# A recurrent layer and a gated attention on one core: the value products move to the head of a step, ScalarE's transfers to 3 + 3 + 2

## The chip, the core and the metric

The kernel runs on one core of a Trainium2 chip. The core has five engines that run side by side and meet through semaphores: TensorE (PE; its weight loads are listed apart as PEld), VectorE (DVE), ScalarE (ACT), GpSimd (POOL) and SyncE (SP, which only issues transfers). Each engine works through its own list of instructions in order: an instruction that waits holds up all that stand behind it on that engine. SP and ACT both issue DMA transfers here.

The metric is the time of one execution in microseconds (us) on the device: the median of the runs. Beside it stands the profile of one execution, in which every instruction has a start and a duration.

## The reference

The input is x (2, 2048, 256) in float32. Two layers follow each other, each behind a layer norm and with its input added back.

```
x = x + rnn(layernorm(x))            # h = tanh(x Wi' + bi + h Wh' + bh), 128 steps and 64 sequences by name;
                                     # here 2 sequences of 2048 steps
q, k = (x @ Wq), (x @ Wk)            # 8 heads of 64
wv   = top2mask(x @ Ws) * sigmoid(x @ Ws)        # per head, 5 experts
v    = sum over e of wv[e] * (x @ Wv[e])
attn = softmax(q k' / 8) v                       # 2048 x 2048 scores per head
out  = sum over e of top2mask(x @ Wd)[e] * (attn @ Wo[e])
x = x + out
```

The second layer has 2 batches x 8 heads, each with 2048 queries against 2048 keys. It fills the span from about 400 us on and is what the change touches.

## The kernel before, in words

The first layer, the gates and the turned inputs are made in the first 400 us. From there one hand-written schedule runs: the block under `tc.manual_schedule()` at the end of the function fixes each engine's order of instructions.

**Units and steps.** A head's queries are cut in four blocks of 512 (`QB`); a head and a block are a unit u, 64 in all. A unit has four steps (`U_T = 4`), each for 128 queries of each of the block's tiles; a step is called W (or t), 256 of them and some more to drain. `T0` is the first step of a head (16 steps a head). In a step the scores come in two parts of 1024 columns. For each part: `scores` (PE, L486) into one of three PSUM buffers, `lowest` (DVE, L500; the scores are negated, so the minimum is what the exponential subtracts), `exponential` (ACT, L510), `turn` (DVE, L522: a transposition within 32 x 32 blocks into a tile `st` that holds two steps; there are two such tiles).

**Deals.** The transposed blocks must also change partitions. `deal` (L537) does that with DMA: sixteen transfers of 128 KB for each pair of steps, from `st` into `pt`, which holds a unit. Eight of them, `LOWER`, go out on SP at an even step right behind `turn(t - 1, 1)`. Eight, `UPPER`, go out on ACT between its exponentials: 3 behind the first exponential of the even step, 2 behind the second, 2 behind the first of the odd step, 1 behind the second. The sixteen are called a wave here, ACT's eight A1 to A8 and SP's S1 to S8. The wave that starts at a step W with W mod 4 = 0 completes a unit; that with W mod 4 = 2 holds its first half.

In the program that is built, the transfers of SP and ACT share eight completion semaphores, given out in turn. A transfer is issued only when the one before it on its semaphore, eight transfers earlier, has landed.

**Products.** `products(u, c)` (L547) multiplies `pt` of a unit with the values `v`, four matrix products a step over four steps (16 in all, each two records in the profile). Every one reads all four steps of the unit, so the first cannot start before the unit's last deal has landed. `LAG = 6` puts the first of unit u at the end of step 4u + 6, behind that step's scores. Then `take` (ACT, L557, at the head of step 4u + 10) brings the result to SBUF, `turn_back` (PE transposes, L597, and an ACT copy `at`, L601, at 4u + 10) turns it, and `close` (POOL, L608 to L624) scales it, applies the output gates and adds it to `y`.

**The lists START, MID and LATE.** Everything else is put with `at(W, place, f, ...)` into a list that the step runs at its head, its middle or its end: `keys` and `queries` of the next head (L398, L414 on PE, copies on ACT; START), `fetch` of stored expert values (SP, L459), `mix` and `mix_sum` (POOL, L469 to L478) that make `v` from them, `weigh` (five small stages on DVE, POOL, ACT that turn minima and sums into weights; `least` is stage 0, `rec` stage 3), and for the last head of a batch `turn_out`, `project_out` and `store` (PE L641, L654, ACT L644 and L647, DVE L661). During heads 2 to 5 of the first batch `experts` (PE L445 on `xs`, which `turned_in` loads with SP; ACT copy L452) makes the expert values of the second batch, two chunks every eight steps, and `keep_experts` stores them.

**One PSUM bank for the small things.** `misc` gives `pk`, `pq`, `pv`, `po`, `py` and `pz` one and the same bank (`bufs=1`). A PE instruction that writes one of them waits until the one before has been read by ACT or DVE. PE's list is in order, so whatever stands behind waits too.

**PE's order at a unit's border** is, by the code before: scores of step 4u + 10 (part 0, part 1), `turn_back(u)`, products of the next unit, START of step 4u + 11 (every fourth unit: `keys`), scores of step 4u + 11.

Of the kernel before, what the change touches and what calls it, by code (L numbers as in the profile page):

```python
# [20 lines left out]
def rnn_then_switchhead_kernel(  # L21
# [336 lines left out]


    U_T = 4  # L360
    LAG = 6
    H_T = NQ * U_T
    G = P // 32
    big = ctx.enter_context(tc.tile_pool(name="big", bufs=2))
# [9 lines left out]
    units = [(i, n) for i in range(len(heads)) for n in range(NQ)]  # L374
# [3 lines left out]
    HC = NCH // 2  # L378

    def weights(i):  # L380
        h = heads[i][1]
        w = ap.tile([P, 2, KC, DH], F32, tag="wqk", name=f"wqk{i}")
        for j, W in enumerate((Wq, Wk)):
            nc.sync.dma_start(
                out=w[:, j], in_=W[:, h * DH : (h + 1) * DH].rearrange("(c p) h -> p c h", p=P)
            )
        w_of[i] = w

    def keys(i, part):

        b, h = heads[i]
        if part == 0:
            k_of[i] = ap.tile([P, 2, QB], F32, tag="k", name=f"k{i}")
        pk = misc([P, 2, HC, 32], f"pk{i}_{part}")
        xc = xT_of[b].rearrange("p k (f c g n) -> p k f g c n", f=2, g=G, n=32)
        for kc in range(KC):
            for o in range(2):
                nc.tensor.matmul(  # L398
                    pk[o * DH : (o + 1) * DH],
                    lhsT=w_of[i][:, 1, kc, :],  # L400
                    rhs=xc[:, kc, part, 2 * o : 2 * o + 2],
                    start=kc == 0,
                    stop=kc == KC - 1,
                )
        nc.scalar.copy(k_of[i][:, part, :], pk.rearrange("p g c n -> p (g c n)"))

    def queries(i, part):

        b, h = heads[i]
        pq = misc([P, QB], f"pq{i}_{part}")  # L410
        for kc in range(KC):
            for o in range(2):
                n = 2 * part + o
                nc.tensor.matmul(  # L414
                    pq[o * DH : (o + 1) * DH, :],
                    lhsT=w_of[i][:, 0, kc, :],
                    rhs=xT_of[b][:, kc, n * QB : (n + 1) * QB],
                    start=kc == 0,
                    stop=kc == KC - 1,
                )  # L420
        q = ap.tile([P, QB], F32, tag="q", name=f"q{i}_{part}")
        qs = ap.tile([P, QB], F32, tag="qs", name=f"qs{i}_{part}")
        nc.scalar.mul(q, pq, -SCALE)
        nc.sync.dma_start(out=qs[0:DH, :], in_=q[DH:P, :])
        nc.sync.dma_start(out=qs[DH:P, :], in_=q[0:DH, :])
        q_of[i, 2 * part] = (q, qs)
        q_of[i, 2 * part + 1] = (qs, q)
# [11 lines left out]
    def experts(b, c):  # L439

        if c % 2 == 0:
            xq_of["x", b, c // 2] = ap.tile([P, 2, DH, E], F32, tag="xq", bufs=3, name=f"xw{b}_{c}")
        pv = misc([P, E, DH], f"pv{b}_{c}")
        for kc in range(KC):
            nc.tensor.matmul(  # L445
                pv.rearrange("p e k -> p (e k)"),
                lhsT=(xT_of[b][:, kc, c * P : (c + 1) * P] if b == 0 else xq_of["s", b, c][:, kc, :]),
                rhs=wv[:, kc].rearrange("p e k -> p (e k)"),
                start=kc == 0,
                stop=kc == KC - 1,  # L450
            )
        nc.scalar.copy(xq_of["x", b, c // 2][:, c % 2], pv.rearrange("p e k -> p k e"))  # L452

    def keep_experts(b, k):
        nc.sync.dma_start(out=xvd[b, k], in_=xq_of.pop(("x", b, k)))
# [86 lines left out]
    def products(u, c):  # L542
        i, _ = units[u]
        if c == 0:
            o_of[u] = ps_o.tile([P, QB], F32, tag="o", name=f"o{u}")
        o = c // HC
        nc.tensor.matmul(  # L547
            o_of[u][o * DH : (o + 1) * DH, :].rearrange("p (g r) -> p g r", r=32),
            lhsT=v_of[i][:, c, :],
            rhs=pt_of[u].rearrange("p g s c r -> p (g s) c r")[:, :, c, :],  # L550
            start=c % HC == 0,
            stop=c % HC == HC - 1,
        )

    def take(u):
        os = ap.tile([P, QB], F32, tag="os", bufs=1, name=f"os{u}")
        nc.scalar.copy(  # L557
            os.rearrange("p (s g r) -> p g s r", g=G, s=U_T),
            o_of.pop(u).rearrange("p (g s r) -> p g s r", g=G, s=U_T),
        )  # L560
        o_of["s", u] = os
        pt_of.pop(u)
# [101 lines left out]
    START, MID, LATE = 0, 1, 2  # L664
    todo = {}

    def at(W, place, f, *a):
        todo.setdefault((W, place), []).append(lambda: f(*a))

    for i, (b, h) in enumerate(heads):  # L670
        T0 = i * H_T
        fresh = h == 0
        if i > 0:
            at(T0 - 13, START, weights, i)
            at(T0 - 5 if fresh else T0 - 9, START, keys, i, 0)
            at(T0 - 4 if fresh else T0 - 7, START, keys, i, 1)
            at(T0 - 3, START, queries, i, 0)
        at(T0 + 4, START, queries, i, 1)
        for n, part in enumerate((0, 4, 1, 5, 2, 6, 3, 7)):
            W = T0 - 3 + n if i == 0 else T0 - 11 + 2 * n  # L680
            at(max(W, 0), LATE, fetch, i, part)
            at(max(W + 2, n), LATE, mix, i, part)
            at(max(W + 2, n), LATE, mix_sum, i, part)
        if h == H - 1 and b + 1 < B:
            at(T0 + 5, LATE, load_turned)
        if h == H - 6 and b + 1 < B:
            for c in range(NCH):
                W = T0 + 8 * (c // 2) + c % 2
                at(W, LATE, turned_in, b + 1, c)
                at(W + 2, START, experts, b + 1, c)  # L690
            for k in range(NCH // 2):
                at(T0 + 8 * k + 4, LATE, keep_experts, b + 1, k)
    for u, (i, n) in enumerate(units):
        b, h = heads[i]
        T1 = u * U_T + LAG + U_T
        for k in range(5):
            at(T1 - 6 + k, LATE, weigh, u, k)
        at(T1, MID, turn_back, u)
        at(T1, LATE, close, u)
        if h == H - 1:  # L700
            for s in range(U_T):
                c = n * U_T + s
                at(T1 + s, LATE, residual_in, b, c)
                at(T1 + 2 + s, START, turn_out, b, c)
                at(T1 + 2 + s, MID, project_out, b, c)
                at(T1 + 3 + s, LATE, store, b, c)

    with tc.manual_schedule():
        weights(0)
        keys(0, 0)  # L710
        queries(0, 0)
        keys(0, 1)
        for c in range(NCH):
            experts(0, c)
            if c % 2 == 1:
                keep_experts(0, c // 2)
        for W in range(NT + LAG + U_T + 8):
            t, u, j = W, (W - LAG) // U_T, (W - LAG) % U_T

            def extra(place):  # L720
                for f in todo.pop((W, place), []):
                    f()

            def upper(a, b, c, d):
                if t % 2 == 0 and 0 < t <= NT:
                    deal(t - 1, nc.scalar, UPPER[a:b])
                if t % 2 == 1 and 1 < t <= NT + 1:
                    deal(t - 2, nc.scalar, UPPER[c:d])

            if j == 0 and 0 < u <= len(units):  # L730
                take(u - 1)
            extra(START)
            if t < NT:
                scores(t, 0)
                lowest(t, 0)
            if 0 < t <= NT:
                turn(t - 1, 1)
                if t % 2 == 0:
                    deal(t - 1, nc.sync, LOWER)
            if t < NT:  # L740
                exponential(t, 0)
                scores(t, 1)
                lowest(t, 1)
            upper(0, 3, 5, 7)
            extra(MID)
            if t < NT:
                turn(t, 0)
                exponential(t, 1)
            upper(3, 5, 7, 8)
            if 0 <= u < len(units):  # L750
                for c in range(2):
                    for o in range(2):
                        products(u, o * HC + 2 * j + c)
            extra(LATE)
        assert not todo, todo.keys()

# [47 lines left out]
```

## Time and profile before

| | us |
|---|---|
| median of 3 runs | 2102.23 |
| runs | 2097.94 to 2102.54 |
| the profiled execution | 2105.63 |
| its span, first to last instruction | 2103.7 |
| PE busy | 1553.8 (74%) |
| DVE busy | 1462.6 (70%) |
| POOL busy | 917.5 (44%) |
| ACT busy | 814.2 (39%) |
| mean granted TensorE clock | 0.844 |

Busy time does not count the issuing of transfers, which holds ACT's list as well. A line of the profile names the source line, the engine, the operation and `out<-in` by the program's names. In an answer on waits, `PE o L547 <- DMA pt<-st: 97.8, 44, 6.9` reads: PE stood idle ahead of line 547 until a deal landed, 97.8 us in total, in 44 places, 6.9 us the longest. In a timeline a line starts with start and duration, and ends in brackets with the idle time ahead of it and what ended it. `xN` merges N neighbours of one kind; `ACTq` and `SPq` are the issuing of transfers.

### The profile page before, as it was taken

What the parts mean: (1) busy time and instruction counts of PE and PEld (TensorE: products, weight loads), DVE (VectorE), ACT (ScalarE), POOL (GpSimd) and SP (SyncE); (2) the same over time, 40 slices, a digit from 0 to 9 for tenths busy, and PEclk for the clock granted to TensorE, in tenths of its full rate; (3) what the DMA queues carried; (4) which work ended last, traced back from release to release, by engine and by line L of the source; (5) the groups of instructions that cost most, each with busy time, mean ns of one, the idle gap of its engine ahead of it and who ended that gap; (6) DMA issues with size and microseconds to landing.
All of it is one profiled execution on the core that took longest, in us unless ns stands there. A gap on an engine that the chain in (4) does not pass through costs nothing.

```text
span 2103.7 us, 21889 instructions
## 1 busy us (share of the span) xinstructions
PE 1553.8 (74%) x6226; PEld 608.0 (29%) x6226; DVE 1462.6 (70%) x2170; ACT 814.2 (39%) x1571; POOL 917.5 (44%) x1150
## 2 busy tenths in 40 slices
PE   5952223777878777777788799888878788878786
PEld 4852222222222222222222233222222222222233
DVE  8667775378766666666777676777778777777750
ACT  2530000345443444444444444444444444444441
POOL 0000000355555555544666544456556556565432
PEclk9975555989888888889899899888889888888897
DMA  3000000478776767776878877777777878777771
GB/s 104 1 14 30 30 30 25 135 203 232 206 194 175 202 182 203 194 189 186 215 202 206 224 206 198 218 207 203 192 205 213 208 205 217 198 193 206 200 202 41
DMA packets 161020, 352.04 MB, mean 167 GB/s; under 512 B 49344, under 2 KB 70656, under 8 KB 160768
## 3 DMA queue, kind: packets, MB, share of 16 engines
q1 hardware_dynamic: 110112, 215.70, 38.1%
q10 hardware_dynamic: 50784, 134.89, 24.1%
q8 instruction: 52, 0.85, 0.2%
q14 instruction: 72, 0.59, 0.1%
HBM read 57.89 MB, written 15.73 MB: 35 GB/s over the span
## 4 chain that ended last, share of the span: by engine, by line
PE 28%; DMA 26%; DVE 23%; SPq 5%; issue 5%; POOL 3%; ACT 3%; ACTq 2%; DVEq 0%; POOLq 0%
DMA pt<-st 23%; PE o L547 10%; DVE low L500 8%; DVE st L522 7%; PE s L486 7%; SPq L537 4%; PE pv L445 2%; ACTq L537 2%; PE pz L654 2%; PE pk L398 2%; DMA xs<-x2d 2%; PE pg L304 1%; ACT e L510 1%; DMA xq<-xvd 1%; PE pq L414 1%
## 5 line engine op out<-in xcount | busy, mean ns | idle before, releaser
L500 DVE TENSOR_REDUCE low<-s 128x1 f32<-128x1024 f32 x512 | 612.6, 1197 | 396.1 <-PE s L486 395.3
L510 ACT ACTIVATE e<-s,low 128x1024 f32<-128x1024 f32 x512 | 571.0, 1115 | 652.0 <-DVE low L500 385.3
L522 DVE STREAM_TRANSPOSE st<-e 128x1024 f32<-128x1024 f32 x512 | 631.3, 1233 | 82.2 <-DMA pt<-st 44.8
L547 PE MATMUL o<-pt,v 128*64 128x512 f32 x2048 | 580.3, 693 | 110.9 <-DMA pt<-st 97.8
L486 PE MATMUL s<-k,q 64*128 64x512 f32 x1024 | 547.7, 652 | 17.6 <-ACT e L510 17.6
L486 PE MATMUL s<-k,qs 64*128 64x512 f32 x1024 | 547.7, 652 | 13.3 <-ACT e L510 13.1
L469 POOL TENSOR_TENSOR xq<-xq,gates_all 128x640 f32<-128x640 f32 x128 | 190.7, 1489 | 399.2 <-DMA xq<-xvd 399.2
L608 POOL TENSOR_TENSOR at<-at,f 128x512 f32<-128x512 f32 x64 | 66.7, 1042 | 496.5 <-ACT at L601 496.5
L547 PEld LDWEIGHTS o<-pt,v 128*64 128x64 f32 x2048 | 142.6, 151 | 441.1 <-issue 405.5
L486 PEld LDWEIGHTS s<-k,q 64*128 64x128 f32 x1024 | 180.0, 200 | 207.1 <-issue 115.2
L486 PEld LDWEIGHTS s<-k,qs 64*128 64x128 f32 x1024 | 180.1, 200 | 194.4 <-issue 101.7
L478 POOL TENSOR_TENSOR v<-v,xq 128x128 f32<-128x128 f32 x384 | 199.8, 520 | 30.1
L624 POOL TENSOR_TENSOR y<-y,pro 128x1280 f32<-128x1280 f32 x56 | 162.4, 2900 | 4.4
L597 PE MATMUL po<-ident,os 128*128 128x128 f32 x256 | 49.3, 323 | 116.1 <-ACT os L557 109.0
L617 POOL TENSOR_TENSOR pro<-at,gates_all 128x1280 f32<-128x1280 f32 x56 | 130.9, 2338 | 4.4
L293 PE MATMUL tpc<-ident,xn 128*128 128x128 f32 x64 | 17.4, 427 | 151.3 <-DVE xn L141 146.0
L510 ACT ACTIVATION_READ_ACCUMULATOR e<-s,low 128x1 f32 x512 | 100.2, 196 | 0.0
L569 POOL TENSOR_TENSOR f<-least,low 128x8 f32<-128x8 f32 x64 | 12.8, 200 | 185.1 <-DVE least L567 185.1
L601 ACT COPY at<-po 128x512 f32<-128x512 f32 x64 | 37.5, 585 | 133.4 <-DMA xq<-xvd 54.1
L597 PEld LDWEIGHTS po<-ident,os 128*128 128x128 f32 x256 | 31.0, 157 | 167.0 <-ACT os L557 149.5
L297 ACT COPY xs<-tpc 128x256 f32<-128x256 f32 x16 | 6.0, 372 | 178.7 <-DVE xT L296 178.7
L398 PE MATMUL pk<-xT,wqk 128*64 128x512 f32 x256 | 66.9, 644 | 9.6 <-DMA wqk<-in_Wk 8.9
(107 smaller groups left out, 1278.1 us busy)
## 6 DMA issues: line engine op xcount, KB each, us to landing
pt<-st ACTq DMA_DIRECT2D x1024, 128.0 KB, 3.6
pt<-st SPq DMA_DIRECT2D x1024, 128.0 KB, 3.8
xq<-xvd SPq DMA_DIRECT2D x128, 320.0 KB, 4.3
qs<-q SPq DMA_DIRECT2D x64, 128.0 KB, 3.2
xvd<-xw SPq DMA_DIRECT2D x16, 320.0 KB, 3.1
x<-in_x SPq DMA_DIRECT2D x16, 256.0 KB, 5.7
x1d<-x SPq DMA_DIRECT2D x16, 256.0 KB, 2.0
z<-x1d SPq DMA_DIRECT2D x32, 128.0 KB, 2.9
```

The lines of the kernel that those rows point to most:

```text
L398: nc.tensor.matmul(pk[o * DH : (o + 1) * DH], lhsT=w_of[i][:, 1, kc, :], rhs=xc[:, kc, part, 2 * o : 2 * o + 2], start=kc == 0, stop=kc == ...
L469: nc.gpsimd.tensor_tensor(xq, xq, w.unsqueeze(2).to_broadcast([P, 2, DH, E]), ALU.mult)
L478: nc.gpsimd.tensor_tensor(v, v, xq[:, :, :, e], ALU.add)
L486: nc.tensor.matmul(ss[:, o, :], lhsT=q_of[i, n][o][half, s * P : (s + 1) * P], rhs=k_of[i][half, part, :], start=True, stop=True,)
L500: nc.vector.tensor_reduce(low_of[u][:, s, part : part + 1], s_of[t, part].rearrange("p o q -> p (o q)"), AX.X, ALU.min,)
L510: nc.scalar.activation(e_of[t, part], s_of.pop((t, part)), AF.Exp, bias=low_of[u][:, s, part : part + 1], scale=-1.0, accum_out=den_of[u][ ...
L522: nc.vector.transpose(st_of[t // 2][:, :, t % 2, part * HC : (part + 1) * HC, :].rearrange("p g c r -> p g (c r)"), e_of.pop((t, part)).re ...
L537: engine.dma_start(out=pt_of[u][32 * k : 32 * (k + 1), g, j : j + 2], in_=st_of[t // 2][32 * g : 32 * (g + 1), k],)
L547: nc.tensor.matmul(o_of[u][o * DH : (o + 1) * DH, :].rearrange("p (g r) -> p g r", r=32), lhsT=v_of[i][:, c, :], rhs=pt_of[u].rearrange("p ...
L597: nc.tensor.transpose(po[:, s].rearrange("p o k -> p (o k)"), os[:, s * P : (s + 1) * P], ident)
L617: nc.gpsimd.tensor_tensor(pr, at[:, :, 0, :].unsqueeze(2).to_broadcast([P, U_T, E, DH]), mask.unsqueeze(3).to_broadcast([P, U_T, E, DH]), ...
L624: nc.gpsimd.tensor_tensor(y, y, pr, ALU.add)
```

## The change

Five things change in the schedule; no instruction is added or taken away.

1. `LAG` is 7 and the products stand at the head of a step, behind START, ahead of the step's scores. On PE their place among the scores is the same as before. What is different: START's work of that step (`keys`, `queries`, `experts`, `turn_out`) now stands ahead of the products, not behind them.
2. `take(u)` stands behind the unit's last products in the same step, 4u + 10, and so behind START's copies on ACT, not ahead of them. The stages of `weigh` come one step later (`T1 - 5 + k`, with the same `T1`).
3. ACT's deals are split 3, 3, 2: A6 goes out ahead of the odd step's first exponential, A7 and A8 right behind it; none behind the second.
4. `fetch`, `mix` and `mix_sum` of the later heads come one step later; `weights` moves from START to LATE of the same step.
5. `experts` comes 5 steps behind `turned_in`, not 2; `keep_experts` 4 steps later than before.

```diff
-    LAG = 6
+    LAG = 7
...
-            at(T0 - 13, START, weights, i)
+            at(T0 - 13, LATE, weights, i)
...
-            W = T0 - 3 + n if i == 0 else T0 - 11 + 2 * n
+            W = T0 - 3 + n if i == 0 else T0 - 10 + 2 * n
...
                 at(W, LATE, turned_in, b + 1, c)
-                at(W + 2, START, experts, b + 1, c)
+                at(W + 5, START, experts, b + 1, c)
             for k in range(NCH // 2):
-                at(T0 + 8 * k + 4, LATE, keep_experts, b + 1, k)
+                at(T0 + 8 * k + 8, LATE, keep_experts, b + 1, k)
...
-        T1 = u * U_T + LAG + U_T
+        T1 = u * U_T + LAG + U_T - 1
         for k in range(5):
-            at(T1 - 6 + k, LATE, weigh, u, k)
+            at(T1 - 5 + k, LATE, weigh, u, k)
...
-            if j == 0 and 0 < u <= len(units):
-                take(u - 1)
             extra(START)
+            if 0 <= u < len(units):
+                for c in range(2):
+                    for o in range(2):
+                        products(u, o * HC + 2 * j + c)
+                if j == U_T - 1:
+                    take(u)
...
-            upper(0, 3, 5, 7)
+            upper(0, 3, 6, 8)
             extra(MID)
             if t < NT:
                 turn(t, 0)
                 exponential(t, 1)
-            upper(3, 5, 7, 8)
-            if 0 <= u < len(units):
-                for c in range(2):
-                    for o in range(2):
-                        products(u, o * HC + 2 * j + c)
+            upper(3, 6, 8, 8)
             extra(LATE)
```

## The prediction

> **What bounds the kernel now.** First the chain that ended last, by line, on the page.
>
> ```profile
> DMA pt<-st 23%; PE o L547 10%; DVE low L500 8%; DVE st L522 7%; PE s L486 7%; SPq L537 4%; PE pv L445 2%; ACTq L537 2%; PE pz L654 2%; PE pk L398 2%; DMA xs<-x2d 2%; PE pg L304 1%; ACT e L510 1%; DMA xq<-xvd 1%; PE pq L414 1%
> ```
>
> No engine is full; the chain alternates between deals in flight and the products behind them. The waits say who stands still meanwhile.
>
> ```profile
> DVE low L500 <- PE s L486: 395.3, 101, 43.1
> ...
> ACT e L510 <- DMA pt<-st: 107.2, 54, 5.6
> PE o L547 <- DMA pt<-st: 97.8, 44, 6.9
> ...
> PE pv L445 <- DMA xs<-x2d: 47.3, 8, 7.7
> ```
>
> The products wait 97.8 us for deals, and VectorE waits 395.3 us for scores, which stand behind those products on TensorE. ScalarE waits too: a deal whose semaphore is not free holds the exponential behind it. Next ScalarE's timeline over one completing wave (released at 1058.74, when VectorE's transposition 1057.51 + 1.23 ended).
>
> ```profile
> 1061.78 0.51 ACTq L537 DMA_DIRECT2D pt<-st  x1
> 1062.40 1.11 ACT L510 ACTIVATE e<-s,low 128x1024 f32<-128x1024 f32 x1 [0.51 <-DVE low L500]
> ...
> 1063.42 1.93 ACTq L537 DMA_DIRECT2D pt<-st  x2
> ...
> 1065.57 0.51 ACTq L537 DMA_DIRECT2D pt<-st  x1
> ...
> 1069.81 0.58 ACT L601 COPY at<-po 128x512 f32<-128x512 f32 x1 [1.47 <-issue]
> ```
>
> The lines are A5, the odd step's exponential, A6 and A7, A8, and the copy that frees the small PSUM bank. By the chain A7 went out at 1064.84, 0.02 us after an earlier deal had landed, and A8 landed at 1069.81. TensorE, the same moment:
>
> ```profile
> 1067.29 0.78 PE L597 MATMUL po<-ident,os 128*128 128x128 f32 x4 [2.50 <-ACT os L557]
> 1069.94 3.68 PE L547 MATMUL o<-pt,v 128*64 128x512 f32 x8 [1.88 <-DMA pt<-st]
> 1073.38 2.46 PE L398 MATMUL pk<-xT,wqk 128*64 128x512 f32 x8
> ```
>
> So a unit is a loop: scores, seven VectorE operations (7 us), a wave (11 us), products (3.7 us), sometimes a projection (2.2 us), scores. It takes 22.6 to 25 us in the plain stretches. VectorE's own work in it is 8 x (1.20 + 1.23) = 19.4 us; it has 3.4 to 5.8 us of slack, all at the unit's border.
>
> **The deals (change 3).** The hope in it is that the last deal lands earlier. A7 cannot leave before 1064.84, when its semaphore comes free. A8 then follows at the issue's 0.51 us, at 1065.37, not 1065.57: 0.2 us earlier. I read twenty more waves the same way: in nearly all A7 is held by S4, S5 or A4, landed 5.9 to 6.8 us into the wave. The price is ScalarE's: A6 left at 1063.42 and not at 1062.30 although ScalarE was free to issue, so it is held too, and now the exponential stands behind it and starts near 1064.0 instead of 1062.40, 1.6 us late. VectorE's slack at the border covers that; uncovered it would cost 1.6 us a unit. Which semaphores meet depends on the new order, which I can't see. Bounds for A8: 0.9 us earlier (if A7 and A8 go straight behind A6 and that exponential) to 0.8 us later (if A7 waits for S6, some 1 us behind S5). I take 0.15 us earlier, the row's nearest, over 30 plain units: **-5 us**, between -27 and +24.
>
> **Products and START (changes 1 and 2).** Ahead of scores nothing changes: products of a unit already stood between the scores of step 4u + 10 and those of 4u + 11. What changes is START.
>
> *Keys at the border.* At step T0 - 9 (mod 4: 3, the border) `keys` now stands ahead of the first products. It looks like free filling of the 1.88 us wait. But `pk` needs the one small bank, and the copy that frees it ran at 1069.81 to 1070.39, later than the products could start. So `pk` waits, and the products, whose deals have landed, wait behind it. The copy also comes later itself: it stands behind the next wave's first three deals, whose transposition is held by the late exponential (0.85 us). So `pk` starts at about 1071.2 where the products had started at 1069.94: 1.3 us. Would TensorE be quicker afterwards? The rows of a busy stretch (1.94 us for eight product records, 1.89 for eight of `pk`) give 3.83 us for both, a gain of 2 us against the 5.83 seen. The Trainium skill, TensorE: Matmul & The Clock Gate, section "What's actually happening", says that the gate opens after a stretch of busy time of about 3.4 us, not after a number of matmuls. Then whichever group comes first is slow and the sum stays 5.83; I take this, since the 3.68 us row above is such a first stretch. Ten heads outside the special stretches: **+13 us** (0 if the copy were early, 20 if it is 2 us late).
>
> *turn_out.* For the last head of the first batch each of 16 steps runs `py` (START), scores, `pz` (MID), products. Here the products filled the time in which VectorE emptied the bank:
>
> ```profile
> 1248.29 1.94 PE L547 MATMUL o<-pt,v 128*64 128x512 f32 x8
> 1250.16 0.55 PE L641 MATMUL py<-ident,y 128*128 128x128 f32 x3
> ```
> ```profile
> 1248.91 0.41 DVE L661 TENSOR_TENSOR z<-pz,z 128x256 f32<-128x256 f32 x1
> 1249.24 1.22 DVE L522 STREAM_TRANSPOSE st<-e 128x1024 f32<-128x1024 f32 x1
> 1251.82 1.22 DVE L500 TENSOR_REDUCE low<-s 128x1 f32<-128x1024 f32 x1 [1.35 <-PE s L486]
> ```
>
> `py` could start when z ends, 1249.32. Now: `py` 1249.35, products 1249.85 to 1251.7, scores 1.0 us later than before; and VectorE is already waiting for these scores (1.35 us). The other steps give 0.75 to 1.5 us. With four such steps in the second batch (the rest is drain, where no scores follow): 20 x 1.0 = **+20 us** (10 to 28).
>
> *take* behind START's copies: only `experts` has one there (0.42 us, eight times), covered by the deals' 2 us. Nothing, or 3 us.
>
> **Experts (change 5).** Before, `pv` comes two steps behind the load of `xs`, which SP issues behind eight deals:
>
> ```profile
> 766.58 2.47 PE L445 MATMUL pv<-wv,xs 128*128 128x320 f32 x4 [5.02 <-DMA xs<-x2d]
> ```
>
> VectorE stood 7.45 us there. The eight units with this take 29.1 to 31.0 us between transpositions that release their waves, against about 24.5 (plus 0.5 for the loads, which stay): 8 x 4.6 = **-37 us** (-30 to -42). With five steps the load is long there.
>
> The new places cost. Steps T0 + 8k + 5 meet `queries` of the next head (T0 - 3) four times: `pv`, then `pq`, one bank. `pq` waits for ScalarE's copy of `pv`, which stands behind A6 of the running wave, some 5.9 us into it; before, `pq` was through by then. Then `pq`, products, scores, and only then the exponential, with A7 and A8 behind it. Scores come 6 to 8 us late; VectorE's slack of 3 us takes part. Here too the idle stretch makes TensorE slow (the `pv` above, 2.47 us behind 5.02 us idle, is 1.34 elsewhere). Some 6 us each: **+24 us** (8 to 30). In four other units the second `pv` waits for the copy of the first, which pushes the step's scores 3 us back, hence the next wave's start and the copy that `keys` needs: 3.5 us each where plain ones cost 1.3: **+14 us** (4 to 18).
>
> **The rest.** `rec` one step later no longer waits for POOL (10.0 us in 13 places, most of it in the stretch that releases a wave): **-8 us** (-12 to 0). `fetch` and the mixing a step later: still two steps ahead of the products that need them, POOL is 44% busy; without that cover 3.7 us a piece (1.49 for the multiplication and 4 x 0.5). SP: `fetch` directly behind the deals instead of behind `queries`' two transfers, `weights` (two issues, 1.6 us) behind both; `keep_experts` 0.58 us. SP stands idle 3 to 10 us ahead of each wave, which hides them; uncovered 2 us a head.
>
> **The sum** against the profiled execution (2105.6): -5 + 13 + 20 - 37 + 24 + 14 - 8 = +21, so 2126.6. I take 5 us off, because the three bank waits (13, 24, 14) were each read in one place and their slack may overlap: +16. The median stands 3.4 us below the profiled run: 2102.2 + 16 = **2118 us**, 0.8% slower.
>
> **The rivals.** (a) *The wave shortens.* If the new order of semaphores lets A8 leave 0.9 us earlier, in all 44 units whose products waited, it gives 44 x 0.9 = 40 us where I put 5: 2118 - 35 = 2083. For it: 97.8 us of waiting is there to win. Against: what holds A7 in the waves I read is a landing, not the exponential. It decides from about 0.5 us a unit (21 / 44).
> (b) *ScalarE becomes the bound.* A6 ahead of the exponential pushes it 1.6 us; if A7 also meets a later landing (0.8 us) VectorE's slack is gone and each of 44 units loses 0.6 us more: 2118 + 26 = 2144. For it: the 107.2 us that exponentials already wait for deals. Against: 3.4 us slack.
> (c) *It cancels*: the experts' gain pays for everything if the four meetings with `queries` cost 8 and turn_out 10: 2118 - 16 = about 2102.
>
> **How the numbers follow.** Forecast 0.55, with its own range 2105 to 2135; (a) 0.25; (b) 0.10; (c) 0.10. 0.2% is 4 us, about what runs of this kernel spread by. Faster: (a) and 0.02 of (c), 0.27; same: the rest of (c), 0.08; slower: forecast and (b), 0.65. The range reaches down to (a) and up past (b): 2078 to 2150.
>
> **What would show it.** After: no line of `pv` waiting for xs; `pk` at a border ending a wait for `at` L601 and products behind it with no wait for deals; `pq` behind `pv` waiting for `xw` L452 four times; `py` ahead of products and `z` L661 as its releaser more often; A8 about 7 us into a completing wave as before. I am wrong if A8 leaves under 6.6 us into the wave, or if `pk` finds the bank free.

## The result, and the profile after

The changed kernel takes 2130.16 us (median of 4 runs, 2119.43 to 2134.81); the kernel before, on the same chip beside it, 2100.09 (2094.87 to 2102.54). The ratio is 1.0139, with a 95% interval of 1.0094 to 1.0185. In a second measurement it was 2121.26 against 2100.24, ratio 1.0104 (1.0068 to 1.0139). So the change costs 21 to 30 us. The profiled execution took 2119.43 us (span 2117.6) against 2105.63: 13.8 us between the two profiles. It is the fastest of its four runs; 7 to 16 us of the slowdown are in no profile.

The chain that ended last, by line, for the kernel after:

```profile
DMA pt<-st 17%; PE o L547 12%; DVE low L500 8%; DVE st L522 7%; PE s L486 7%; ACTq L537 4%; DMA xq<-xvd 3%; ACT e L510 3%; PE pk L398 2%; SPq L537 2%; PE pq L414 2%; PE pv L445 2%; PE pg L304 1%; PE pz L654 1%; DMA qs<-q 1%
```

Its waits (in total, places, longest):

```profile
DVE low L500 <- PE s L486: 432.9, 113, 44.7
...
ACT e L510 <- DMA pt<-st: 56.8, 36, 4.5
...
PE pk L398 <- ACT at L601: 35.8, 14, 3.5
...
PE pq L414 <- ACT xw L452: 24.0, 4, 6.3
...
PE py L641 <- DVE z L661: 19.0, 18, 1.5
...
PE o L547 <- DMA pt<-st: 16.2, 14, 1.8
```

The wait for deals fell by 82 us, the experts' wait for `xs` is gone, exponentials wait half as long for deals, and yet VectorE waits 38 us longer for scores. In place of the waits removed stand three for the small bank. The page's row of L547 says the same with every cause together: its idle time went from 110.9 to 47.8 us.

On TensorE as a whole the idle time (span less busy) fell from 549.9 to 541.8 us, and the busy time of the same 6226 instructions rose from 1553.8 to 1575.8; in the second profile they are 541.0 and 1570.3. So the waits mostly changed place, and some instructions run slower. The largest part is `pk`, by the groups of instructions of before and of after (count | busy, mean ns | idle ahead):

```profile
L398 PE MATMUL pk<-xT,wqk 128*64 128x512 f32 x256 | 66.9, 644 | 9.6 <-DMA wqk<-in_Wk 8.9 <-ACT q L423 0.7
L398 PE MATMUL pk<-xT,wqk 128*64 128x512 f32 x256 | 86.5, 812 | 46.6 <-ACT at L601 35.8 <-DMA wqk<-in_Wk 8.7 <-DVE z L661 1.4
```

The mean granted clock did not fall (0.844 before, 0.845 after). What changed is which work stands in the stretches at half clock (granted clock 0.50): behind 400 us they hold 303 us of TensorE's busy time before, 334 after and 325 in the second profile. The next rows show one.

A completing wave in the stretch with `keys` at the border, released at 1034.33. ScalarE's timeline, kernel after:

```profile
1037.36 1.83 ACTq L537 DMA_DIRECT2D pt<-st  x2
1039.29 1.11 ACT L510 ACTIVATE e<-s,low 128x1024 f32<-128x1024 f32 x1 [1.81 <-DVE st L522]
...
1040.36 1.36 ACTq L537 DMA_DIRECT2D pt<-st  x2
...
1046.24 0.59 ACT L601 COPY at<-po 128x512 f32<-128x512 f32 x1 [1.62 <-issue]
```

TensorE's, the same border:

```profile
1043.56 1.11 PE L597 MATMUL po<-ident,os 128*128 128x128 f32 x4 [1.89 <-ACT os L557]
1046.88 3.47 PE L398 MATMUL pk<-xT,wqk 128*64 128x512 f32 x8 [2.20 <-ACT at L601]
1050.18 1.88 PE L547 MATMUL o<-pt,v 128*64 128x512 f32 x8
```

A5 and A6 leave ahead of the exponential, A7 and A8 straight behind it. A8 goes out 6.88 us into the wave and the last of ScalarE's deals lands at 11.01, that is at 1045.3. The products could start there. They start at 1050.18: `pk` stands ahead and waits 2.20 us for `at`, then takes 3.47 us. The granted clock is 0.50 from 1043.18 to 1050.00, over nearly all of `pk`, and 1.00 behind it; in the prediction's rows of before the half-clock stretch (1067.68 to 1074.51) lay over the products. The products start 4.8 us late, but the unit does not lose as much, because `pk` is done by then: from the first record to the last the two groups take 5.18 us here and 5.90 before.

To set sizes against each other I cut each profile at the transpositions that release a completing wave and summed the lengths of units 1 to 62 by what is in them. The first three columns are units in the stretch of `experts`: 8 in which the kernel before waited for `xs`, 4 in which chunks meet `queries`, 4 others. Then 6 units with `turn_out`, the 8 other units with `keys` at the border, and 32 without. All in us.

| | xs wait | meetings | others | turn_out | keys | rest | all |
|---|---|---|---|---|---|---|---|
| before | 237.1 | 100.1 | 106.8 | 168.9 | 200.4 | 775.8 | 1589.1 |
| after | 188.7 | 117.0 | 114.2 | 206.9 | 206.9 | 767.9 | 1601.6 |
| after, second measurement | 186.8 | 116.7 | 117.7 | 209.8 | 209.3 | 758.1 | 1598.5 |
| products first | 190.3 | 109.9 | 96.4 | 169.6 | 199.9 | 761.4 | 1527.5 |
| turn_out behind | 186.8 | 116.8 | 115.0 | 175.1 | 211.8 | 758.8 | 1564.4 |
| keys behind | 190.6 | 116.4 | 101.4 | 203.5 | 203.8 | 759.0 | 1574.7 |
| meetings apart | 191.8 | 96.9 | 112.3 | 211.5 | 213.8 | 764.4 | 1590.8 |
| first and apart | 189.7 | 89.4 | 97.6 | 175.0 | 202.6 | 752.4 | 1506.7 |

The two profiles of the changed kernel differ by up to 3.5 us in the first five columns and by 9.8 under "rest"; across the runs that leave the work of the `keys` units alone (the two of after, turn_out behind, meetings apart) that column moves by 6.9. Differences smaller than these are not read from a single pair of rows.

### The profile page after: what moved, and what is told of

Its sections match the earlier page's. It is cut to its first block, busy times and chain, and to the rows that moved or that the text cites. A ratio compares the mean times of both kernels' runs of the same rounds, so it can differ in the third digit from the quotient of the medians.

```text
span 2117.6 us, 21988 instructions
## 1 busy us (share of the span) xinstructions
PE 1575.8 (74%) x6226; PEld 607.5 (29%) x6226; DVE 1464.6 (69%) x2170; ACT 815.6 (39%) x1571; POOL 919.1 (43%) x1150
## 4 chain that ended last, share of the span: by engine, by line
PE 30%; DVE 23%; DMA 23%; issue 5%; ACT 4%; ACTq 4%; POOL 2%; SPq 2%; POOLq 0%; DVEq 0%
DMA pt<-st 17%; PE o L547 12%; DVE low L500 8%; DVE st L522 7%; PE s L486 7%; ACTq L537 4%; DMA xq<-xvd 3%; ACT e L510 3%; PE pk L398 2%; SPq L537 2%; PE pq L414 2%; PE pv L445 2%; PE pg L304 1%; PE pz L654 1%; DMA qs<-q 1%
## 5 line engine op out<-in xcount | busy, mean ns | idle before, releaser
L547 PE MATMUL o<-pt,v 128*64 128x512 f32 x2048 | 573.1, 686 | 47.8 <-DMA pt<-st 16.2
L469 POOL TENSOR_TENSOR xq<-xq,gates_all 128x640 f32<-128x640 f32 x128 | 190.3, 1487 | 609.6 <-DMA xq<-xvd 609.6
L547 PEld LDWEIGHTS o<-pt,v 128*64 128x64 f32 x2048 | 148.0, 153 | 377.3 <-issue 342.3
L569 POOL TENSOR_TENSOR f<-least,low 128x8 f32<-128x8 f32 x64 | 12.8, 199 | 340.0 <-DVE least L567 340.0
L398 PE MATMUL pk<-xT,wqk 128*64 128x512 f32 x256 | 86.5, 812 | 46.6 <-ACT at L601 35.8
L414 PE MATMUL pq<-xT,wqk 128*64 128x512 f32 x256 | 71.1, 682 | 27.4 <-ACT xw L452 24.0
L601 ACT COPY at<-po 128x512 f32<-128x512 f32 x64 | 37.5, 585 | 113.6 <-issue 44.7
```

What stands on the lines that cost most here:

```text
L398: nc.tensor.matmul(pk[o * DH : (o + 1) * DH], lhsT=w_of[i][:, 1, kc, :], rhs=xc[:, kc, part, 2 * o : 2 * o + 2], start=kc == 0, stop=kc == ...
L414: nc.tensor.matmul(pq[o * DH : (o + 1) * DH, :], lhsT=w_of[i][:, 0, kc, :], rhs=xT_of[b][:, kc, n * QB : (n + 1) * QB], start=kc == 0, sto ...
L469: nc.gpsimd.tensor_tensor(xq, xq, w.unsqueeze(2).to_broadcast([P, 2, DH, E]), ALU.mult)
L547: nc.tensor.matmul(o_of[u][o * DH : (o + 1) * DH, :].rearrange("p (g r) -> p g r", r=32), lhsT=v_of[i][:, c, :], rhs=pt_of[u].rearrange("p ...
```

## The experiments

Times are medians, each with the ratio to the kernel before on the same chip and its 95% interval. Differences between runs are between medians of several chips, on which the kernel before took 2098.5 to 2100.6 us; where the changed kernel is one side, two figures are given, one for each of its measurements.

### START behind the products (changed kernel)

```diff
-            extra(START)
             if 0 <= u < len(units):
...
                 if j == U_T - 1:
                     take(u)
+            extra(START)
```

> The changed kernel with one thing put back: at the head of a step the products (and take) stand ahead of START again, everything else as changed. Theory (one small PSUM bank: what START waits for now holds the products and the scores): the turn_out units go back from 36 us to 29 us each (4 x 7 plus 3 for the one before, and 7 in the second batch), the border units with keys give back about 1 us each (10), the four meetings of experts and queries lose only the products' share (2 us each): about 2130 - 55 = 2075 to 2090, under the kernel before. Rival (ScalarE's later exponentials are the price): nothing of this changes them, the time stays at 2115 or more.

Measured: 2054.36 us (2042.07 to 2060.88, 4 runs), ratio 0.976 (0.9713 to 0.9807). That is 67 to 76 us faster than the changed kernel and 46 us faster than before. The waits of this run:

```profile
DVE low L500 <- PE s L486: 357.3, 105, 44.7
...
PE o L547 <- DMA pt<-st: 23.1, 20, 2.5
...
PE pq L414 <- ACT xw L452: 17.2, 4, 4.5
```

The lines of `pk` for `at` and of `py` for `z` are gone, VectorE's wait is 76 us shorter, and of the 74 us between the two profiles' sums by unit 37 are in the units with `turn_out`, 18 in the others of `experts`, 7 with `keys`, 7 in the meetings. A8 leaves 6.86 us into a wave and lands at 11.08, as after. So the loss comes from the place of START ahead of the products, not from ScalarE's deals: the rival in which ScalarE becomes the bound falls here. `take` moved with the products in this run; what it has of the gain alone was not measured. The gain is larger than I expected, so the parts of START together had been sized too low.

### turn_out alone behind the products

```diff
-    START, MID, LATE = 0, 1, 2
+    START, MID, LATE, NEXT = 0, 1, 2, 3
...
-                at(T1 + 2 + s, START, turn_out, b, c)
+                at(T1 + 2 + s, NEXT, turn_out, b, c)
...
                 if j == U_T - 1:
                     take(u)
+            extra(NEXT)
```

> The changed kernel with turn_out alone put behind the products again (keys, queries and experts stay ahead of them). Theory: the six units with turn_out in them took 206.9 us against 168.9 before and 169.6 with all products first, so this alone gives 37 us: about 2093. Rival (the wait for the bank is only moved from the products to turn_out): 2115 or more.

Measured: 2086.24 us (2081.82 to 2096.95, 9 runs), ratio 0.9951 (0.9927 to 0.9975). 35 to 44 us come back; the units with `turn_out` shrink from 206.9 to 175.1. TensorE in the changed kernel over the two steps that lose most:

```profile
1240.34 0.63 PE L597 MATMUL po<-ident,os 128*128 128x128 f32 x4 [1.46 <-DVE z L661]
1241.70 0.90 PE L641 MATMUL py<-ident,y 128*128 128x128 f32 x3 [0.73 <-ACT at L601]
1242.53 3.68 PE L547 MATMUL o<-pt,v 128*64 128x512 f32 x8
1246.14 1.22 PE L486 MATMUL s<-k,q 64*128 64x512 f32 x1
...
1252.08 1.94 PE L414 MATMUL pq<-xT,wqk 128*64 128x512 f32 x8 [1.37 <-DVE z L661]
1254.80 0.52 PE L641 MATMUL py<-ident,y 128*128 128x128 f32 x3 [0.79 <-ACT q L423]
1255.25 1.94 PE L547 MATMUL o<-pt,v 128*64 128x512 f32 x8
1257.12 0.69 PE L486 MATMUL s<-k,qs 64*128 64x512 f32 x1
```

The same border in the kernel before:

```profile
1255.69 0.66 PE L597 MATMUL po<-ident,os 128*128 128x128 f32 x4 [1.30 <-DVE z L661]
1256.27 1.94 PE L547 MATMUL o<-pt,v 128*64 128x512 f32 x8
1258.14 0.55 PE L641 MATMUL py<-ident,y 128*128 128x128 f32 x3
```

And a plain step with `turn_out` behind:

```profile
1239.09 1.76 PE L654 MATMUL pz<-wo,yT 128*128 128x256 f32 x6
1240.77 1.94 PE L547 MATMUL o<-pt,v 128*64 128x512 f32 x8
1242.64 0.55 PE L641 MATMUL py<-ident,y 128*128 128x128 f32 x3
1243.12 0.69 PE L486 MATMUL s<-k,qs 64*128 64x512 f32 x1
```

From scores to scores the border step takes 10.94 us in the changed kernel (1235.20 to 1246.14) and 7.98 before (1250.64 to 1258.62), the step with `pq` 10.99 (1246.14 to 1257.13) and 8.50 before (1258.62 to 1267.12), and a plain step 7.39 (1257.13 to 1264.52) and 5.95 before (1238.38 to 1244.33), which is also what the plain step with `turn_out` behind takes. So a step loses 1.4 us where it is plain, 2.5 with `pq` and 3.0 at the border. A single step waits twice for the bank: 1.46 or 1.37 us for `z`, then 0.73 or 0.79 for a copy of ScalarE. At the border eight product records then take 3.68 us and the first scores 1.22, where they take 1.94 and 0.69 elsewhere: the granted clock is 0.50 from 1241.15 to 1247.98. In the plain step with `turn_out` behind no instruction waits: the products fill the time in which `z` is made.

### keys alone behind the products

```diff
-            at(T0 - 5 if fresh else T0 - 9, START, keys, i, 0)
+            at(T0 - 5 if fresh else T0 - 9, NEXT, keys, i, 0)
```

(with the same `NEXT` as above, and `turn_out` back in START)

> The changed kernel with the first half of keys alone put behind the products again. Theory: pk at the border waits for the bank and holds products whose deals have landed; ten plain units give back 8 us together, the four with experts 12: about 2110. Rival (keys fill an idle stretch, which costs nothing): 2130, within 5.

Measured: 2096.27 us (2081.86 to 2111.07, 20 runs), ratio 0.9995 (0.9975 to 1.0015). `keys` at the border costs 25 to 34 us, more than I expected of it alone. By unit its largest share is 12.8 us in the other units of `experts`; 3.1 are in those with `keys` only, 3.4 in `turn_out` and 8.9 in the rest, each within what two profiles differ. The `keys` units are better read from all rows: with `keys` behind the products they take 199.9 to 203.8 us (before, products first, keys behind, first and apart), with `keys` ahead 206.9 to 213.8, so about 1 us a unit.

### The meetings put apart

```diff
-                at(W + 5, START, experts, b + 1, c)
+                at(W + 5 + c // 2 % 2 * (1 + c % 2), START, experts, b + 1, c)
```

> The changed kernel with every other pair of experts one step and three steps later (steps 14 and 16 of a head's sixteen, not 13 and 14), so that none meets queries of the next head. Theory: the four units of 29.3 us go back to 25: 2130 - 17 = 2113. Rival (the second product in a unit costs this wherever it stands): 2125 or more.

Measured: 2101.43 us (2089.31 to 2108.02, 20 runs), ratio 1.0018 (1.0001 to 1.0034): 20 to 29 us back, where I expected 17. The column of the meetings falls from 117.0 to 96.9, and no other falls by more than it differs between profiles (`keys`, which this run does not touch, rises by 6.9); no `pq` waits for `xw` any more. What happens in a meeting, first on TensorE in the changed kernel:

```profile
985.10 3.64 PE L414 MATMUL pq<-xT,wqk 128*64 128x512 f32 x8 [6.32 <-ACT xw L452]
988.56 1.89 PE L547 MATMUL o<-pt,v 128*64 128x512 f32 x8
```

then ScalarE, with the copy that frees the bank:

```profile
983.43 1.09 ACTq L537 DMA_DIRECT2D pt<-st  x1
984.62 0.42 ACT L452 COPY xw<-pv 128x320 f32<-128x320 f32 x1 [1.43 <-POOL v L478]
988.78 0.60 ACT L423 ACTIVATE q<-pq 128x512 f32<-128x512 f32 x1 [3.74 <-PE pq L414]
992.88 1.11 ACT L510 ACTIVATE e<-s,low 128x1024 f32<-128x1024 f32 x1 [3.50 <-DVE low L500]
```

and VectorE:

```profile
991.56 1.23 DVE L500 TENSOR_REDUCE low<-s 128x1 f32<-128x1024 f32 x1 [9.45 <-PE s L486]
```

The copy `xw` stands behind A6 on ScalarE, `pq` behind the copy (and at a granted clock of 0.50), products and scores behind `pq`, and VectorE stands 9.45 us. The exponential with A7 and A8 behind it comes at 992.88.

### Experts in the kernel before, alone

```diff
-                at(W + 2, START, experts, b + 1, c)
+                at(W + 5, START, experts, b + 1, c)
...
-                at(T0 + 8 * k + 4, LATE, keep_experts, b + 1, k)
+                at(T0 + 8 * k + 8, LATE, keep_experts, b + 1, k)
```

> The kernel before with the experts' move alone: five steps behind their load, stored four steps later. Theory: -48 us in eight units, and of the meetings with queries about 3.5 us each come (products are already through there) and about 2 us in the four units with keys: 2100 - 48 + 22 = 2074. Rival (the time goes to the same place in another form): within 10 us of 2100.

Measured: 2086.80 us (2083.26 to 2091.68, 5 runs), ratio 0.9933 (0.9909 to 0.9957): 14 us faster, half of what I expected. The units that waited for `xs` give 34.7 us, but the four meetings take 21.2 back, although START still stands behind the products here. So the meetings belong to the new places of `experts`, whatever the place of START.

### Experts two steps behind the load again, in the changed kernel

The same two lines, the other way round: `W + 2` and `+ 4`.

> The changed kernel with the experts two steps behind their load, and stored four steps earlier, as before. Theory: the eight units get their wait for the load back (6 us each, 48 together) and the meetings with queries and keys go (17 and 7): 2130 + 24, some 2150; more if the second chunk, now ahead of the border's products, holds them too. Rival (the transfer is hidden anyway, the moved experts gain nothing): 2130 or less.

Measured: 2189.79 us (2185.48 to 2198.77, 4 runs), ratio 1.0431 (1.0394 to 1.0468), 60 to 69 us slower than the changed kernel. Its waits:

```profile
DVE low L500 <- PE s L486: 499.0, 105, 43.0
...
PE pv L445 <- DMA xs<-x2d: 66.4, 8, 10.3
```

The load's wait is back and longer than the 47.3 us of before. These eight units take 286.0 us, against 188.7 with five steps and 237.1 before, twice the loss I expected: in this order the products stand behind the waiting `pv`. Once START stands ahead, two steps are too few; three and four were not tried.

### The deals alone

In the changed kernel, back to 3, 2, 2, 1:

```diff
-            upper(0, 3, 6, 8)
+            upper(0, 3, 5, 7)
...
-            upper(3, 6, 8, 8)
+            upper(3, 5, 7, 8)
```

> The changed kernel with ScalarE's deals dealt out as before, 3 + 2 + 2 + 1. Theory: what holds the last deals is the landing eight transfers earlier, so the split moves A8 by 0.2 us and the time by 10 us at most: 2120 to 2140. Rival (a deal ahead of the exponential costs ScalarE 1 us a unit, and that is the slowdown): 2105 or less.

Measured: 2136.64 us (2127.5 to 2137.96, 4 runs), ratio 1.015 (1.0115 to 1.0184). It is not faster, so the split was not what cost the time. The traces show what held the deals: in the changed kernel A7 left within 0.06 us of the landing of S4 in all of 40 plain waves, and A8 within 0.06 us of such a landing (mostly S5) in 37. In the kernel before A7 was held in all 40, A8 in 20. And in the kernel before, to 3, 3, 2 (the same lines reversed):

> The kernel before with the deals' split 3 + 3 + 2 alone. Theory (A7 and A8 are held by the landing eight transfers earlier): between -12 and 0 us, the products still wait about 90 us for deals. Rival (the last deal really leaves half a step earlier): -30 or more. Rival (ScalarE's exponential, pushed by A6, becomes the bound): slower than 2104.

Measured: 2093.45 us (2087.34 to 2099.97, 11 runs), ratio 0.9964 (0.9944 to 0.9984), 7 us faster. One part of the expectation missed, that the products would still wait some 90 us for deals:

```profile
PE o L547 <- DMA pt<-st: 26.8, 22, 7.0
```

A 71 us smaller wait and 7 us of gain: in the middle (median) of 38 plain units the last deal lands at 10.92 us into the wave instead of 11.17 and the products start at 11.29 instead of 11.50. 38 x 0.2 is the 7 us. The rest of the wait went because the transposition `po` just ahead of the products ends at 10.28 instead of 9.62. TensorE is idle earlier instead: its scores wait 67.5 us for exponentials, which A6 has made late, where they waited 30.7 (its wait ahead of `po` is not longer: 103.2 for `os`, 109.0 before). In the changed kernel the landing is at 11.04 and the first products, again in the middle, start at 11.46.

### The small stages alone

`weigh`, `fetch`, `mix`, `mix_sum` and `weights` at their new places, in the kernel before:

```diff
-            at(T0 - 13, START, weights, i)
+            at(T0 - 13, LATE, weights, i)
...
-            W = T0 - 3 + n if i == 0 else T0 - 11 + 2 * n
+            W = T0 - 3 + n if i == 0 else T0 - 10 + 2 * n
...
-            at(T1 - 6 + k, LATE, weigh, u, k)
+            at(T1 - 5 + k, LATE, weigh, u, k)
```

> The kernel before with weigh, fetch and mix one step later and the weights' load behind them, nothing else. Theory: the wait of rec for POOL, 10 us, goes; fetch now stands directly behind the deals: -3 to -12 us. Rival (POOL's mixing now delays close, and with it the unit's end): slower than 2104.

Measured: 2107.39 us (2100.78 to 2119.27, 12 runs), ratio 1.0036 (1.0017 to 1.0056): 7 us slower where I expected a gain. My theory fell. SP's timeline over a completing wave of a unit with `queries` (released at 1818.6 in both), first before, then here:

```profile
1824.31 0.56 SPq L424 DMA_DIRECT2D qs<-q  x1
1825.20 0.63 SPq L425 DMA_DIRECT2D qs<-q  x1
1826.17 0.40 SPq L459 DMA_DIRECT2D xq<-xvd  x1
```

```profile
1824.36 0.49 SPq L459 DMA_DIRECT2D xq<-xvd  x1
1824.95 0.50 SPq L424 DMA_DIRECT2D qs<-q  x1
1826.18 0.49 SPq L425 DMA_DIRECT2D qs<-q  x1
```

`fetch` (320 KB, by the page's list of issues) now leaves 5.75 us into the wave, ahead of A8 at 7.35, where it left at 7.5, behind it. In the middle of the nine plain units of this kind A8 then takes 5.01 us from issue to landing instead of 3.96, and the last of ScalarE's deals lands at 12.49 instead of 11.32. That is 9 x 1.17 = 10.5 us. It is not the read alone: in 27 other plain units of the kernel before, without `queries`, `fetch` also left ahead of A8 (5.69 us into the first of these waves), and there A8 took 4.10 us in the middle and the landing was at 11.16. With the two query transfers ahead and `fetch` behind (6 units before) A8 took 3.90, with `fetch` and one or both of them ahead 4.6 to 5.1 (3 units before, 9 here). The next run leaves `fetch`, the mixing and `weights` where they were and moves `weigh` alone:

```diff
-            at(T1 - 6 + k, LATE, weigh, u, k)
+            at(T1 - 5 + k, LATE, weigh, u, k)
```

> The kernel before with the stages of weigh one step later, nothing else (fetch, mix and the weights' load stay). With these four together the time rose by 7 us. Theory (fetch, 320 KB, now issued ahead of the queries' transfers, lands the last deals 1.2 us later in the units with queries; the later rec is worth something): below 2101, by up to 10. Rival (the later weigh itself costs, over POOL or ScalarE): 2107, as the four together.

Measured: 2089.00 us (2078.85 to 2098.5, 12 runs), ratio 0.9945 (0.9922 to 0.9968), 10 us faster; in the units with `queries` the landing is at 11.24, and the wait of `rec` for `tot` falls from 10.0 to 0.7 us. So `weigh` gains what I said, and the other moves of this part cost 17 to 19 us, of which the transfers' order explains 10.5 (by length, the nine units take 11.9 us more than in this run). What the rest is, and whether `mix` or `weights` has a part in it, I did not separate.

### Both repairs

START behind the products and the meetings apart, that is the diffs of the first and the fourth experiment together, in the changed kernel.

> Products ahead of START as in the first experiment, and the experts' pairs apart from queries as in the one before this. Theory: 2054 less what is left of the four meetings, 27.5 us a unit against 24: 2054 - 13 = 2041. Rival: 2054, within 5.

Measured: 2031.32 us (2026.06 to 2034.95, 4 runs), ratio 0.968 (0.9654 to 0.9705). It beats the kernel before by 3.2% and the changed one by 4.2 to 4.6%. It is 10 us under what I expected: the meetings give 20.5 us by unit against products first, not 13. The chain of this run:

```profile
DMA pt<-st 22%; PE o L547 12%; DVE low L500 8%; PE s L486 6%; DVE st L522 6%; DMA xq<-xvd 4%; ACTq L537 3%; SPq L537 2%; PE pz L654 2%; PE pk L398 2%; DMA qs<-q 2%; ACT e L510 2%; PE pg L304 1%; PE pq L414 1%; PE pv L445 1%
```

It is again bound by deals in flight and products behind them, as before.

### The changed kernel again

> The changed kernel once more, for its spread and a second profile: 2119 to 2135, median about 2130; the units with turn_out again some 7 us longer than before, the eight units with the load some 6 us shorter.

This is the second measurement given with the result (2113.12 to 2127.30, span 2111.3). Its row in the table repeats the first within 3.5 us in every column but "rest".

## Why the prediction was right, and where not

The direction and the mechanism were right: one bank, with START ahead of the products. The forecast was +16 against 2102.2; measured are +21 and +30. That the sum came so near is partly luck: turn_out was sized 15 to 24 us too small, the load's gain 11 too small and the meetings 7 too large, and these errors partly cancel.

- **What would show it.** All signs came: no `pv` waits for `xs`; `pk` ends a wait for `at` L601 and the products behind it have none; `pq` waits for `xw` four times; `py` stands ahead of the products with `z` as releaser; A8 leaves 7.00 us into a wave (median of the plain ones), not under 6.6. The rival of the shortened wave is out.
- **Deals, -5.** Alone, -7. That a landing holds A7 was right. The size was lucky: A8 could not have left at 1065.37, because in the row shown it was itself held until S5 landed at 1065.55. What moved is A7: in the new order it shares its semaphore with S4 in all plain waves and leaves 5.85 us into the wave, not 6.38; A8 then waits for S5 or A5 and leaves 0.25 us earlier. The exponential starts 4.96 us into the wave instead of 4.49, 0.5 us late in the middle, where I read 1.6 from one wave: A6 was held by A3 there, and in the new order it follows S2, which lands sooner.
- **Keys at the border, +13, and four other units, +14.** Together 27; taken out together they give 25 to 34. The split between them is less sure: taking `keys` out lowers the two columns by 3.1 and 12.8, and all rows together give about 1 us for a unit with `keys` only, where I put 1.3; outside the special stretches nine heads have such a unit, not ten. Of the two readings of the clock the slower one was nearer: from the first record to the last `pk` and the products took 5.18 us, against 5.90 before (the prediction has 5.83) and 3.83 in the busy rows. The half-clock stretch is 6.83 us long in both, whichever group stands in it; it ended 4.57 us after the first of these records before and 3.12 us after it here.
- **turn_out, +20.** This term was mis-sized: the column rises by 38 us, and taking it out gives 35 to 44 in time. I put 1.0 us on each of 20 steps from one plain step. Plain steps lose 1.4; at the border and at the step with `pq`, where the bank changes hands three times in a row, it is 3.0 and 2.5, the border partly from a half-clock stretch that I had not seen coming.
- **Experts, -37, and meetings, +24.** Measured in the columns -48 and +17. The meetings were sized a little high. The load's gain is 34.7 with the experts alone, as forecast; the other 13 come with the split of the deals: in the changed kernel with the old split this column is 208.3, against 186.8 to 191.8 in the seven rows of the table with the new one. By itself, with the wait for `xs` still there, the split leaves it at 240.4. By what path it helps in these units was not traced.
- **fetch, mix and weights, 0.** In the kernel before this term failed. I wrote that SP stands idle ahead of each wave and that this hides the new places. SP's own time is hidden; the transfers are not, because in the units with `queries` the read and a query transfer are in flight at the same time as A7 and A8. There the group costs 17 to 19 us. In the changed kernel I see less of it: `fetch` also leaves ahead of `queries`, at 6.46, but the query transfers mostly leave behind A8, which takes 4.21 us, and the landing is at 11.06, against 3.74 and 10.72 with the split of deals alone. What the group costs in the changed kernel was not measured.
- **weigh, -8.** Alone, -10.
- **The 5 us taken off for overlap** had no ground in the runs. Deals, `weigh`, the group of `fetch` and the experts by themselves give -7 - 10 + 18 - 14 = -13; START ahead adds the rest. But with START behind, the kernel gained 46 us, so the parts do not add. Two pieces of the difference are named above: the 13 us that the split adds in the units of the load, and the delay by `fetch` that is small in the changed kernel. No run measures them apart, so the rest stays open. Open too is why the profiled execution lies below its median.
- **Rival (c)** was summed wrongly: with meetings at 8 and turn_out at 10 it would be 26 us under the forecast, 2092, and not 16. Measured by unit are 17 and 38.

## What to carry to other kernels

What is put ahead of waiting work on an in-order engine brings its own waits with it: look not only for idle time there, but for when the buffer that the moved instruction writes comes free, and on which queue the copy that frees it stands. A large total of waits for one cause is not what can be gained; here 71 us of it went for 7, because work ahead of it came later. A transfer costs nothing on its queue and may still delay the ones that the path waits for, so its place among them counts.

## What the runs showed of the hardware

How long a transfer takes depends on what was issued just ahead of it: the last 128 KB deal took 4.10 us with a 320 KB read ahead of it, 3.90 with two query transfers of 128 KB, and 5.09 with the read and one query transfer (middle of 27 and 6 units of the kernel before, and of 6 with the small stages later).

TensorE can go to half clock behind short waits, but does not each time. In the changed kernel it waited 1.46 us ahead of `po` and 0.73 us behind it, the granted clock was 0.50 for 6.83 us, and eight product records took 3.68 us. With `turn_out` behind, it waited 1.38 us ahead of the same `po` and 0.73 us behind it (1255.32 to 1256.71), and the clock stayed at 1.00; a single wait of 1.37 us later in that run (ahead of 1271.77) was followed by 0.50 for 3.41 us. So the length of the wait alone does not decide it in these runs.
